# Tying a side chain's indirect transfers to the main chain's latest ScalarE instruction

## The chip, the cores and the metric

One Trainium2 chip; the kernel runs on one of its cores. The metric is device time in microseconds (us) of one execution. The kernel before takes 2101.95 us, the median of 15 runs (2098.95 to 2109.45).

## What is computed

Four layers on x of shape (4, 1024, 128), float32, each an attention-like part and a feed-forward part with a residual sum and a layer norm after each. Cut to what matters here:

```python
x = layernorm(x + L0_attn(x)); x = layernorm(x + L0_ffn(x))   # a scan; a quantised 128x128 product
x = layernorm(x + L1_attn(x))                                 # a linear state-space recurrence
x = layernorm(x + L1_ffn(x))      # 16 experts, 4 of them for each token, and a shared one
x = layernorm(x + L2_attn(x))     # causal softmax, 16 heads of 8
x = layernorm(x + L2_ffn(x))      # 8 experts, 2 for each token
x = layernorm(x + L3_attn(x))     # a Toeplitz mix with a gate
x = layernorm(x + L3_ffn(x))      # 32 experts, 4 for each token, and a shared one
```

An expert layer adds to each token the outputs of its chosen experts, each times a weight from the router.

## The kernel before

**Tiles.** The 4 x 1024 tokens lie in 32 tiles of 128 tokens in x, [128, 32, 128] in SBUF. Layer 1's experts take them in two halves, `a` and `r` (16 tiles each); layer 2's in `a2` (16), `m2` and `n2` (8 each); layer 3's in `a` (16), `b` and `c` (8 each).

**One expert layer.** The router's products give logits; `positions` (L1272 writes the result, `posl1r` and the like) gives each token the row that it has in a list sorted by expert. `spread` (L1303) copies every token's row of x to its places in that list in DRAM, named l1rr for layer 1, half r: for each tile and each of its k choices one indirect transfer of 128 rows of 512 bytes. 16 tiles with 4 choices are 64 transfers. The experts read the list in groups of four tiles (`gathered`, L1322; the load is L1326, on SP). Each load waits for all scatters of the list. Its tile xg is transposed on TensorE (L165, tp), multiplied with weights that lie in SBUF (L157, gu, yp), and the results go to a second list (l1yr). `collect` (L1350) gathers from that one: k indirect transfers fill a tile yt, and k VectorE instructions (L1361) add yt times the router's weight to x.

**Indirect transfers.** All are issued on GpSimd (POOL) by `indirect` (L1292; its instruction has line L1295), in the order in which they are emitted. `collect` keeps as many yt tiles as its pool has buffers (5 in layer 1, 8 in layers 2 and 3); a gather into a buffer waits for the adds that read it before. `moved_by` is the time at which the planner thinks that the transfers are over, 1.26 us for one.

**Who sets the order.** Stages are Python generators. One emits instructions and yields the time that it thinks they take. `mix(main, side)` (L233) takes a step of main, then steps of side until main's time is used up; when main has ended it emits all the rest of side, unless `drain=False`. `queued` (L223) emits one step of the side chain and puts an ordering "queued behind" on each of its instructions, behind main's latest one on the same engine (`self.latest`, of PE, ScalarE, VectorE and POOL). That is an order only and no wait: where an engine has none of main's work, its side work starts as soon as its data is there. POOL has none in the stages of this change. `run` (L217) adds the yields to `self.now`. In `collect` the adds of a tile are emitted when `self.now` has reached `moved_by` + 4.0, and where it has not, the generator yields 1.0 at a time.

**The stages that the change touches,** in order of time, in `all`:

- closing half a of layer 1 (`l1_close(a)`: gather, add, norm) beside the tail of half r's layers 0 and 1 (scans on VectorE, L645);
- **A**: `l2_attn(0)`, main, with `l1_route(r)` and the 64 scatters of l1rr at its side. Main's ScalarE work is the exponential (L1051, pr); L1057 masks pr on VectorE. Half r's experts come next, and with them eight wall loads for layer 2 (768 KB each, SP, L1437);
- **B**: half r's experts in layer 1, with layer 2's route of a2 and its 32 scatters (l2ra) at the side;
- **C**: layer 2's experts of a2, with `l1_close(r)` at the side: 64 gathers of l1yr in two quarters, adds, norm, transposes;
- `l2_attn(1)` and layer 2's other experts, with layer 2's gathers (`rows_in`) and layer 3's attention and route at the side;
- layer 3's experts of a, b, c. Beside those of a: `rows_in(m2)`, `rows_in(n2)`, `l3_attn(b)`, `l3_route(b)`, then the scatters of l3rb; main yields 9.0 for each block of its shared expert (L1652) and 3.7 for each group of the others (L1730). Behind l3rb stand on POOL the gathers of l3ya, the scatters of l3rc and the gathers of l3yb.

Of the kernel before, what the change touches and what calls it, by code (L numbers as in the profile page):

```python
# [56 lines left out]
class Part:  # L57
# [3 lines left out]
    def __init__(self, name, q0, nq, rows=None, lg0=None):  # L61
        self.name, self.q0, self.nq, self.lg0 = name, q0, nq, lg0
        if rows is None:
            self.order = list(range(q0 * QT, (q0 + nq) * QT))
        else:
            self.order = [tile_of(b, 2 * q + k) for b in rows for q in range(q0, q0 + nq) for k in range(2)]
        self.t0, self.nt = q0 * QT, len(self.order)
# [7 lines left out]
class Kernel:  # L75
    def __init__(self, ctx, tc, ins, out, cols, consts, rows):
        self.tc, self.nc, self.ins, self.out = tc, tc.nc, ins, out
        self.count = itertools.count()
        nc = self.nc
        self.const = self.pool(ctx, "const")  # L80
        self.small = self.pool(ctx, "small", 3)
        self.routes = self.pool(ctx, "routes")
        self.side = self.pool(ctx, "side", 2, space=PSUM)
        dram = self.pool(ctx, "dram", space=DRAM)

        self.cols_t = self.load(self.const, ins["cols"])
        self.cst_t = self.load(self.const, ins["consts"])
        self.x = self.tile(self.const, [P, NT, D], "x")
        self.xT = self.tile(self.const, [P, NT * P], "xT")
        nrow = ins["rows"].shape[1]  # L90
        self.rows_t = self.tile(self.const, [P, nrow], "rows")
        nc.gpsimd.dma_start(out=self.rows_t, in_=ins["rows"].to_broadcast([P, nrow]))
        self.col = {k: self.cols_t[:, a:b] for k, (a, b) in cols.items()}
        self.cst = {k: self.cst_t[:, a:b] for k, (a, b) in consts.items()}
        self.row = {k: self.rows_t[:, a:b] for k, (a, b) in rows.items()}
        self.ident = self.cst["ident"]
        self.eps = self.tile(self.const, [P, 1], "eps")
        nc.vector.memset(self.eps, LN_EPS)
        self.halfpi = self.tile(self.const, [P, 1], "halfpi")
        nc.vector.memset(self.halfpi, math.pi / 2)  # L100
        self.ones = self.tile(self.const, [P, E3], "ones")
        nc.vector.memset(self.ones, 1.0)
        self.mhalf = self.tile(self.const, [P, QT], "mhalf")
        nc.vector.memset(self.mhalf, -0.5)
        self.zero = self.tile(self.const, [P, D], "zero")
        nc.gpsimd.memset(self.zero, 0.0)
        self.flag = self.tile(self.const, [1, 1], "flag", I32)
        self.hm = self.tile(self.const, [P, 4], "hmg")

        self.first, self.rest = Part("a", 0, 2), (Part("b", 2, 1), Part("c", 3, 1))  # L110
        self.parts = (self.first, *self.rest)
        self.by_rows = (
            Part("a", 0, 2, range(B), 0), Part("m", 2, 2, (0, 1), NT // 2), Part("n", 2, 2, (2, 3), 3 * NT // 4)
        )

        self.rows_done = 0

        self.listed = set()

        self.traced, self.latest = nc.cur_bb.bb.instructions, {}  # L120
        self.now = self.moved_by = 0.0
        self.moved = []

        self.lists, self.route = {}, {}
        self.both = (self.first, Part("r", 2, 2))
        for lay, ne, k in (("l1", E1, K1), ("l2", E2, K2), ("l3", E3, K3)):
            for pt in {"l1": self.both, "l2": self.by_rows, "l3": self.parts}[lay]:
                tl = -(-((pt.nt * P * k + (P - 1) * ne) // P) // 4) * 4
                self.lists[lay, pt.name] = (
                    self.tile(dram, [tl * P, D], f"{lay}r{pt.name}"), self.tile(dram, [tl * P, D], f"{lay}y{pt.name}"), tl  # L130
                )
        self.wall2 = self.tile(dram, [P, E2 * 3 * F2], "wall2")
        self.xsave = self.tile(dram, [P, NT, D], "xsave")

        self.ksave = self.tile(dram, [P, B, BLK], "ksave")
        self.vsave = self.tile(dram, [P, B, 4, (NH + 1) * VW], "vsave")
# [85 lines left out]

    def queued(self, side):  # L223

        n = len(self.traced)
        got = next(side, None)
        behind = mybir.DependencyInfo(mybir.DependencyClass.NoSync, mybir.DependencyReason.DATA)
        for i in self.traced[n:]:
            if i.engine in self.latest:
                self.tc.add_manual_dep(i, self.latest[i.engine], behind, reason="queued behind")  # L230
        return got

    def mix(self, main, side, pace=1.0, drain=True):  # L233
# [1073 lines left out]
    def spread(self, lay, part, k):  # L1307

        pos, _, _, done = self.route[lay + part.name]
        rows = self.lists[lay, part.name][0]  # L1310
        for t in range(part.nt):
            for i in range(k):
                ins = self.indirect(
                    apart=done,
                    out=rows, out_offset=bass.IndirectOffsetOnAxis(ap=pos[:, t, i : i + 1], axis=0),
                    in_=self.x[:, part.order[t], :], in_offset=None,
                )
                done.append(ins)
            yield (1.26 * k,)
        self.listed.add(lay + part.name)  # L1320

    def gathered(self, pool, rows, g, done, want):  # L1322
# [27 lines left out]
    def collect(self, lay, part, k, yp, first=0, nt=None):  # L1350

        nc = self.nc
        pos, wk, _, _ = self.route[lay + part.name]
        assert f"made {lay}{part.name}" in self.listed
        ys = self.lists[lay, part.name][1]
        late = []

        def add():
            t, yt, _ = late.pop(0)
            for i in range(k):  # L1360
                nc.vector.scalar_tensor_tensor(  # L1361
                    self.x[:, part.order[t], :], yt[:, i, :], wk[:, t, i : i + 1], self.x[:, part.order[t], :],
                    ALU.mult, ALU.add,
                )

        for t in range(first, first + (nt or part.nt)):
            yt = self.tile(yp, [P, k, D], "yt")
            for i in range(k):
                self.indirect(
                    out=yt[:, i, :], out_offset=None, in_=ys,  # L1370
                    in_offset=bass.IndirectOffsetOnAxis(ap=pos[:, t, i : i + 1], axis=0),
                )

            late.append((t, yt, self.moved_by + 4.0))
            if len(late) == yp.bufs:
                while late[0][2] > self.now:
                    yield (1.0,)
                add()
            yield (1.26 * k,)
        while late:  # L1380
            while late[0][2] > self.now:
                yield (1.0,)
            add()
            yield (0.36 * k,)
# [439 lines left out]
    def all(self):  # L1824
# [4 lines left out]
        with ExitStack() as ctx:  # L1829
# [21 lines left out]
                    self.run(self.mix(self.abreast(self.l2_weights(), side), self.l1_close(a, yp)))  # L1851
            with ExitStack() as c2:
                wall = self.l1_wall(c2)
                self.run(self.mix(self.l2_attn(0), self.chain(self.l1_route(r), self.spread("l1", r, K1))))
                wall2 = self.l2_wall(c2)
                yp = self.pool(c2, "l1yr", 5, right=True)
                self.run(self.mix(self.chain(self.l1_experts(r, wall), self.l1_shared(r)), self.routed(a2)))
                self.run(self.mix(self.l2_experts(a2, wall2), self.l1_close(r, yp)))
            listed = lambda name: lambda: name in self.listed
            on = self.served(  # L1860
                self.chain(self.rows_in(a2), self.onward(a, True)),
# [212 lines left out]
```

## Time and profile before

| what | us or share |
|---|---|
| median of 15 runs | 2101.95 (2098.95 to 2109.45) |
| the profiled execution, its own time | 2102.99 |
| its span, first to last instruction | 2101.1 |
| mean granted TensorE clock | 0.888 |
| busy: PE, VectorE, ScalarE, POOL | 1625.9 (77%), 1344.2 (64%), 829.0 (39%), 777.1 (37%) |
| scatters of l1rr (64), first and last start | 704.9 and 787.7 |
| scatters of l2ra (32) | 869.4 to 908.5 |
| gathers of l1yr (64) | 922.6 to 1044.1 |
| scatters of l3rb (32) | 1804.7 to 1845.6 |

Times in the trace count from the span's start. A line of the chain of waits or of a timeline gives start, duration, engine, line, operation and tile; brackets give the idle time before it and what ended it. In a line of a group, the durations are minimum, median and maximum in ns, then follow the first and last start. "POOL" is GpSimd, "DVE" VectorE, "ACT" ScalarE, "SPq" SyncE's issues. An indirect transfer's time on POOL is the time that it keeps POOL; the data lands later.

### The profile page before, as it was taken

What the parts mean: (1) busy time and instruction counts of PE and PEld (TensorE: products, weight loads), DVE (VectorE), ACT (ScalarE), POOL (GpSimd) and SP (SyncE); (2) the same over time, 40 slices, a digit from 0 to 9 for tenths busy, and PEclk for the clock granted to TensorE, in tenths of its full rate; (3) what the DMA queues carried; (4) which work ended last, traced back from release to release, by engine and by line L of the source; (5) the groups of instructions that cost most, each with busy time, mean ns of one, the idle gap of its engine ahead of it and who ended that gap; (6) DMA issues with size and microseconds to landing.
All of it is one profiled execution on the core that took longest, in us unless ns stands there. A gap on an engine that the chain in (4) does not pass through costs nothing.

```text
span 2101.1 us, 28678 instructions
## 1 busy us (share of the span) xinstructions
PE 1625.9 (77%) x9605; PEld 1003.2 (48%) x9605; DVE 1344.2 (64%) x3801; ACT 829.0 (39%) x1193; POOL 777.1 (37%) x701
## 2 busy tenths in 40 slices
PE   6562677688848785999979787987989989788680
PEld 2232433377424343866643233333656678476470
DVE  8766699566666865645654756656583467778263
ACT  4720047233314352433327554663323254443140
POOL 5523148501660470353423000200216710477725
PEclk9775588899878997999989989999999999999895
DMA  9940000233451113432231000003115243155341
GB/s 308 286 124 0 1 19 34 95 96 105 148 175 42 44 67 138 142 116 73 80 124 30 1 1 1 20 2 136 51 47 210 62 129 109 64 140 142 104 136 51
DMA packets 225735, 192.05 MB, mean 91 GB/s; under 512 B 17008, under 2 KB 204272, under 8 KB 225072
## 3 DMA queue, kind: packets, MB, share of 16 engines
q1 hardware_dynamic: 204880, 147.28, 22.2%
q0 software_dynamic: 20704, 42.86, 6.7%
q8 instruction: 83, 1.36, 0.3%
q14 instruction: 68, 0.56, 0.1%
HBM read 93.47 MB, written 96.60 MB: 90 GB/s over the span
## 4 chain that ended last, share of the span: by engine, by line
PE 43%; DVE 17%; issue 7%; POOL 6%; DMA 4%; ACT 2%; SPq 0%; DVEq 0%; POOLq 0%; ACTq 0%
PE gu L157 13%; PE s L157 10%; PE yp L157 6%; PE sc L157 6%; PE tp L165 5%; POOL yt L1295 3%; DVE pr L1057 1%; POOL l3rb L1295 1%; ACT pr L1051 1%; POOL l3rc L1295 1%; PE s L165 1%; DVE x L205 1%; PE pu L157 1%; PE pg L157 1%; DVE y L1592 1%
## 5 line engine op out<-in xcount | busy, mean ns | idle before, releaser
L1051 ACT ACTIVATE pr<-sc 128x1024 f32<-128x1024 f32 x288 | 279.1, 1021 | 216.6 <-PE sc L157 212.1
L157 PE MATMUL gu<-ld,xgT 128*128 x768 | 197.7, 401 | 19.6 <-DVE hg L1693 13.3
L157 PE MATMUL sc<-qm,kT 32*128 32x512 f32 (+3 forms) x1536 | 188.8, 548 | 1.0 <-ACT pr L1051 1.0
L157 PE MATMUL s<-pr,va 128*32 128x512 f32 (+3 forms) x1536 | 163.1, 519 | 17.9 <-DVE x L989 7.3
L157 PE MATMUL gu<-wall,xgT 128*128 x352 | 169.7, 606 | 2.7 <-ACT xgT L167 2.0
L157 PEld LDWEIGHTS gu<-ld,xgT 128*128 128x128 f32 x768 | 143.6, 198 | 46.5 <-issue 10.4
L1057 DVE TENSOR_TENSOR pr<-pr,ld 128x512 f32<-128x512 f32 (+1 forms) x160 | 92.5, 581 | 84.7 <-ACT pr L1051 84.1
L1693 DVE TENSOR_TENSOR hg<-sg,gu 128x256 f32<-128x256 f32 x192 | 78.8, 417 | 105.7 <-ACT sg L1692 105.1
L169 DVE COPY hT<-tp 128x512 f32<-128x512 f32 x140 | 96.0, 686 | 64.7 <-PE tp L165 64.7
L167 ACT COPY xgT<-tp 128x512 f32<-128x512 f32 x118 | 69.0, 586 | 160.3 <-PE tp L165 160.3
L157 PEld LDWEIGHTS sc<-qm,kT 32*128 32x128 f32 x1536 | 82.7, 194 | 98.1 <-issue 60.2
L1692 ACT ACTIVATE sg<-gu 128x256 f32<-128x256 f32 x192 | 72.8, 383 | 142.3 <-PE gu L157 112.2
L165 PEld LDWEIGHTS tp<-ld,hg 128*128 128x128 f32 x736 | 92.3, 142 | 57.3 <-issue 37.6
L1295 POOL DMA_INDIRECT l1ra<-x,posl1a x64 | 94.6, 1478 | 61.0 <-DVE posl1a L1272 41.8
L1466 ACT ACTIVATE sg<-gu 128x512 f32<-128x512 f32 x88 | 52.5, 597 | 162.2 <-PE gu L157 158.6
L165 PE MATMUL tp<-ld,hg 128*128 128x128 f32 x736 | 113.7, 276 | 3.5 <-DVE hT L169 3.4
L157 PE MATMUL yp<-ld,hT 128*128 x768 | 102.5, 277 | 1.8 <-DVE mv L192 1.5
L1295 POOL DMA_INDIRECT l1rr<-x,posl1r x64 | 64.8, 1012 | 99.5 <-DVE posl1r L1272 80.3
L165 PE MATMUL tp<-ld,xg 128*128 128x128 f32 x472 | 76.6, 288 | 31.1 <-DMA xg<-l3rc 13.2
L1468 DVE TENSOR_TENSOR hg<-sg,gu 128x512 f32<-128x512 f32 x88 | 60.0, 682 | 57.0 <-ACT sg L1466 56.8
L157 PEld LDWEIGHTS yp<-ld,hT 128*128 128x128 f32 x768 | 94.1, 193 | 2.7 <-issue 2.0
L157 PE MATMUL yp<-wall,hT 128*128 x704 | 93.1, 276 | 1.5 <-DVE hT L169 1.5
(433 smaller groups left out, 3454.3 us busy)
## 6 DMA issues: line engine op xcount, KB each, us to landing
wall<-wall SPq DMA_DIRECT2D x16, 768.0 KB, 8.5
l3ra<-zero SPq DMA_DIRECT2D x1, 6144.0 KB, 30.4
ld<-in_l_w SPq DMA_DIRECT2D x2, 3072.0 KB
wall<-we SPq DMA_DIRECT2D x24, 256.0 KB, 2.0
ld<-in_l_w SPq DMA_DIRECT2D x1, 6144.0 KB, 20.4
xg<-l3ra SPq DMA_DIRECT2D x24, 256.0 KB, 2.8
l3ya<-yg SPq DMA_DIRECT2D x24, 256.0 KB, 2.3
l1ra<-zero SPq DMA_DIRECT2D x1, 5120.0 KB, 20.2
```

Source lines behind the costliest of these rows:

```text
L157: return self.nc.tensor.matmul(out, lhsT, rhs, start=start, stop=stop)
L165: nc.tensor.transpose(pt[:, k * P : (k + 1) * P], s, self.ident)
L167: nc.scalar.copy(dst, pt[:, : n * P])
L169: nc.vector.tensor_copy(dst, pt[:, : n * P])
L205: nc.vector.tensor_scalar(x, x, mv[:, t, 0:1], rstd[:, t : t + 1], ALU.subtract, ALU.mult)
L1051: nc.scalar.activation(pr, sc[h], AF.Exp)
L1057: nc.vector.tensor_tensor(d, d, cst["tril"].unsqueeze(1).unsqueeze(1).to_broadcast([P, 2, n, P]), ALU.mult)
L1295: ins = self.nc.gpsimd.indirect_dma_start(**kw)
L1466: nc.scalar.activation(sg, gu[:, 0, :], AF.Silu)
L1468: nc.vector.tensor_tensor(h, sg, gu[:, 1, :], ALU.mult)
L1692: nc.scalar.activation(sg, pg[:, :, 0, :], AF.Silu)
L1693: nc.vector.tensor_tensor(h[:, 2 * c : 2 * c + 2, :], sg, pg[:, :, 1, :], ALU.mult)
```

## The change

A flag `gated` is true during stages A, B and C. While it is, each indirect transfer that `queued` emits gets, besides its order, a real (semaphore) wait on the ScalarE instruction of main that was emitted last. And `spread` and `collect` now yield 1.26 after each transfer, everywhere in the kernel, where they yielded 1.26 k after the k transfers of a tile. In `collect` these yields stood behind the adds of an older tile; now they stand ahead of them.

```diff
@@ def queued(self, side):
         for i in self.traced[n:]:
             if i.engine in self.latest:
                 self.tc.add_manual_dep(i, self.latest[i.engine], behind, reason="queued behind")
+            if self.gated and i.name == self.moved[-1]:
+                after = mybir.DependencyInfo(mybir.DependencyClass.Sync, mybir.DependencyReason.DATA)
+                self.tc.add_manual_dep(i, self.latest[mybir.EngineType.Activation], after, reason="in step")
@@ def spread(self, lay, part, k):
                 done.append(ins)
-            yield (1.26 * k,)
+                yield (1.26,)
@@ def collect(self, lay, part, k, yp, first=0, nt=None):
                     in_offset=bass.IndirectOffsetOnAxis(ap=pos[:, t, i : i + 1], axis=0),
                 )
+                yield (1.26,)
...
                 add()
-            yield (1.26 * k,)
@@ def all(self):
+                self.gated = True
                 self.run(self.mix(self.l2_attn(0), self.chain(self.l1_route(r), self.spread("l1", r, K1))))
...
                 self.run(self.mix(self.l2_experts(a2, wall2), self.l1_close(r, yp)))
+            self.gated = False
```

The instructions, their number and POOL's order stay the same; ScalarE's, VectorE's and TensorE's instructions stand in another order from some points on.

More of the change, by code (lines that the diff above doesn't have):

```diff
@@ L1858, in all @@
                 self.run(self.mix(self.l2_experts(a2, wall2), self.l1_close(r, yp)))
+            self.gated = False
             listed = lambda name: lambda: name in self.listed
```

## The prediction

> **What bounds the kernel now.** I read the page first, then the chain of waits by stage, then the tiles that the change gates.
>
> ```profile
> span 2101.1 us, 28678 instructions
> ...
> ## 4 chain that ended last, share of the span: by engine, by line
> PE 43%; DVE 17%; issue 7%; POOL 6%; DMA 4%; ACT 2%; SPq 0%; DVEq 0%; POOLq 0%; ACTq 0%
> ```
>
> No engine bounds it alone; POOL is only 6% of the chain. So transfers matter where the chain crosses them, and the change must be priced stage by stage. First crossing: the lists of the second half of the tokens in layer 1 (l1rr), as the tile's view gives them.
>
> ```profile
> L1295 POOL DMA_INDIRECT l1rr<-x,posl1r x64: 954/958/1447, 704.9 to 787.7; - x64
> ...
>   PE tp L165: 10.4, 1
> ...
> DMA to landing us min/median/max: 2.7/2.8/13.7
> ```
>
> The 64 scatters start 1.26 us apart (0.96 busy, 0.30 issue), from 704.9 to 787.7, under the attention of layer 2. Who needs them is in the chain of waits at the end of that stage:
>
> ```profile
> 810.65 1.01 ACT pr L1051
> ...
> 820.71 0.70 DVE x L989
> 821.44 0.49 DVE bn L191 x2
> 825.31 15.03 DMA xg<-l1rr
> 840.38 1.97 PE tp L165 x8
> ```
>
> ScalarE's last pr of the stage ends at 812.6. The reads of l1rr (L1326) go out at 825.31 on SP, behind the eight 768 KB wall loads issued from 820.71, and land only at 840.4: between 819 and 837 the DMA view shows 380 to 430 GB/s in nearly every slice. So today the wall load ends that wait, and the scatters have landed 35 us early. PE has nothing else: 3.03 us busy in 825 to 840.
>
> Second crossing, layer 3, third quarter of rows (l3rb), from POOL's timeline and then the chain:
>
> ```profile
> 1804.65 0.99 POOL L1295 DMA_INDIRECT l3rb<-x,posl3b  x1 [111.84 <-DVE posl3b L1272]
> ```
> ```profile
> 1845.58 2.21 DMA l3rb<-x,posl3b
> ...
> 1972.18 2.92 DMA xg<-l3rc
> 1975.23 1.98 PE tp L165 x8
> ```
>
> POOL waits for the positions until 1804.65 and then works without a gap to 2012.7: 159.5 us of transfers (64 yt of l3ya, 32 l3rb, 32 l3rc, 32 yt of l3yb) and 48.6 us of idle, nearly all issue, fill the 208 us. The last quarter's experts wait for it at 1972. What delays posl3b delays the end.
>
> **Stage A (l2_attn(0) over the scatters of l1rr): +17.5 us.** The planner's yields, the number of transfers (64) and POOL's order stay. What is new is a real wait. Before, a scatter emitted late still ran early, since nothing on POOL held it. Now each waits for the ScalarE instruction that was main's latest when it was emitted. Following the emission: scatters 1 to 32 get pr instructions that end between 738.5 and 807.7 in the trace of before. From the 33rd on there is no newer one: 18 are emitted in main's last yields (projection, norm), which hold no ScalarE work, and 14 when main has ended. All 32 wait for the pr that ends at 812.6. Then they run in the burst: 32 x 1.264 = 40.4 us, the last begins near 851.8 and lands 2.8 later (median), 854.7. SP's reads wait for all 64; issue to landing is 2.8 (median of xg): the first tp comes at about 857.9 against 840.4, so +17.5. The wall load is by then over and hides nothing. Queued behind the waiting POOL instruction are only the scatters of l2ra (869.4 before), with positions that are themselves side work.
>
> Unknown: 13 to 16 of the 32 run beside the wall load; no row shows that pair. Low end: the quiet period, 1.264, and a read that lands 1 us sooner, 16.5. High end: the l1ra scatters, which averaged 1.478 busy against 1.012 for l1rr: 16 x 0.47 = 7.5 more, and a first read 2 us later: 27. I take the low row's period, since those of l1rr in the same stage are the nearest.
> A rule that speaks against the change: the Trainium skill ("DMA: Bandwidth & Descriptors", SWDGE vs HWDGE vs iDMA) says that each DMA engine takes turns between the queues fed by GpSimd and those fed by hardware. By it the scatters would pass a wall load in turn and only the wall, no longer last, would be late: the sum stays; l1ra's landings of up to 20.2 us beside other loads speak for less than that.
>
> Does the stage itself gain by thinner traffic? Split by whether a transfer runs beside it, the pr of L1057 takes 585 ns with and 578 without on average (median 681 both), L1051 1021 both. At 7 ns for 64 transfers, under 0.5 us: 0.
> The skill's "SBUF — State Buffer" (SBUF: two separate sides) has VectorE and GpSimd exclude each other on a shared port for whole instructions. If each of 64 transfers had held VectorE for its 0.96 us, 61 us would come back; the rows above show none of it, and it is POOL that is slowed (2.82 and 2.14 us beside two scans of L645 at 571 to 576).
>
> **Stage B (l2ra, 32 scatters): 0.** Gates end 6.7 to 12.3 us after the old starts, the last at 916.7; last landing near 922, its reader at 943.7. 20 us of cover.
>
> **Stage C (gathers of l1yr): +0.3 (0 to +5).** PE is 100% busy from 950 to 1050. The first quarter's gates reach 988.4, its adds stood at 998.6; second quarter's last gathers start near 1048.5, land at 1051, adds at 1053.6. Cover 1.3 to 2.7 us. If it fails, the norm and transposes slip one group, at most 5.
>
> **Yields after each transfer, everywhere: +7.2 us.** In `collect` the adds now come after the yields. Four places where that moves something:
> - Closing the first half in layer 1: a tile's four adds go from 562.7 behind both L645 scans (576.4), so POOL's gather of 569.92, which needs that buffer, starts near 576.6. It would have run beside the scans slowly anyway (2.82 and 2.14 instead of 0.94): net +1.7 (0 to +3.5). The chain runs along POOL there (564.9 to 623.6).
> - Start of l2_attn(1): one or two adds of l2ya less ahead of rot (a 9.8 us wait for yt): -1.
> - Layer 3, first quarter of experts (main) over rows_in, l3_attn(b), l3_route(b): the adds slip past main's 9.0 yields, so l3_attn(b) begins three main yields later (10 instead of 7), its route at 27 instead of 24. One such yield takes 3.54 us (gu groups at 1736.67, 1740.21): 10.6 later into the route, now 1782.5 to 1804.2, 21.7 us, of which some 8 are VectorE work of main interleaved. Positions are emitted after main's end, so part of the 8 falls away. posl3b is 4 to 11 later; I take +9, nearer the row of yields. Then POOL's gapless 208 us passes it on.
> - Last quarter of experts: adds of l3yb now hold VectorE ahead of main (PE stalls of 2.05 at 2011.65 and 1.58 at 2022.19, with 1.54 of waiting for yt); they come a group later: -2.5 (-4 to 0).
>
> 1.7 - 1 + 9 - 2.5 = +7.2.
>
> **Sum.** 17.5 + 0 + 0.3 + 7.2 = +25.0 on the profiled execution's 2102.99 us, 2128; that execution is 1.04 above the median of 2101.95, so 2127 for a median.
>
> **Rivals.**
> 1. Only the drained burst counts: layer 3's route makes up its delay (POOL's order has slack that I missed, or VectorE is freer). Against it: POOL shows no gap. 25 - 9 + 1 = +17: 2119.
> 2. The drained scatters collide with the wall load, +9.5 more: 2136.5; stage C's cover failing too, +5: 2142. For it: l1ra's slow scatters; against: the median landing of 2.8 in this stage.
> 3. Not slower: bursts cost the neighbours more than the rows say, through shared ports and DMA engines. Place: stages A to C, where 160 transfers are thinned. To cancel +25 each must give back 25/160 = 0.16 us of path; the rows show 0.007, at most 1.1 us. Priced at the break-even it gives 2102, and it decides from 0.16 us on.
> 4. The gate doesn't bind: if the tail of scatters were released before 812.6 (an earlier ScalarE instruction than I followed), up to 12 us later than now would still be hidden, and only the yields count: +7: 2109.
>
> **How the numbers follow.** Forecast (+25, 2120 to 2132) 0.50; rival 1 0.20; rival 2 0.17; rival 4 0.05; rival 3 0.08, half of it within 0.2% and half faster. 0.2%, about 4.2 us, is what a measurement here can tell from no change. Slower 0.91 with rival 4 mostly in it, same 0.05, faster 0.04. Range 2112 to 2142: low end 16.5 in stage A, nothing in layer 3, gains full (16.5 + 0 - 1 - 4 = +11.5, near 2113); high end 27 + 5 + 3.5 + 11 - 1 - 2.5 = +43, of which I keep +40.
>
> **What would show it.** Right: l1rr scatters to about 852 with an idle POOL that ends on ACT pr L1051, the first tp of l1rr near 858, all later starts moved by that; posl3b some 9 us later beyond the shift. l2ra and l1yr readers not waiting for POOL. Wrong: tp at 840 with scatters finished, a scatter period well above 1.3 after 820, L1057 shorter than 0.58, or PE waiting for adds between 990 and 1060.

## The result and the profile after

The changed kernel takes 2135.57 us (median of 9 runs, 2129.04 to 2143.81) against 2102.86 (47 runs of the kernel before): 1.0156 times, 95% interval 1.0142 to 1.0171, or +32.7. The prediction was 2127 and 2112 to 2142. The profiled execution took 2133.36, which is 30.4 above the one of before. In the lines shown, line numbers have moved by 1 to 5.

The page of the changed kernel:

```profile
span 2131.5 us, 28726 instructions
...
PE 35%; DVE 11%; issue 5%; POOL 4%; DMA 3%; ACT 2%; SPq 0%; DVEq 0%; POOLq 0%; ACTq 0%
```

Its shares of the chain add up to 60% (79% before), so the two can't be laid side by side. What can are the stages. The tile l1rr, and then the chain of waits behind stage A:

```profile
L1300 POOL DMA_INDIRECT l1rr<-x,posl1r x64: 953/958/1301, 741.1 to 856.3; - x64
...
  ACT pr L1056: 146.2, 9
...
  PE tp L166: 27.5, 1
...
DMA to landing us min/median/max: 2.7/2.7/3.4
```
```profile
856.34 2.21 DMA l1rr<-x,posl1r
858.55 0.02 SPq L1331
...
858.68 2.82 DMA xg<-l1rr
...
861.54 2.02 PE tp L166 x8
```

GpSimd waited 146 us for ScalarE's pr, and the last scatter begins at 856.3 instead of 787.7. What was a wait of 15 us behind the wall load is now a chain of the last scatter, its landing, SP's issue and the read of the list, each with nothing in between. (The row "DMA to landing" is that of the reads: the trace records no landing of a scatter of l1rr. The last one's, 2.21 us, is from the chain.) Layer 3's scatters of l3rb, GpSimd's timeline:

```profile
1834.72 0.99 POOL L1300 DMA_INDIRECT l3rb<-x,posl3b  x1 [120.16 <-DVE posl3b L1277]
```

They wait for posl3b, 120.16 us instead of 111.84. In closing half a of layer 1 a wait has appeared that the trace of before doesn't have. First the fifth and sixth gather of the row before, then the third to fifth after:

```profile
569.92 0.94 POOL L1295 DMA_INDIRECT yt<-l1ya,posl1a  x1 [0.30 <-DVE b L641]
571.17 2.82 POOL L1295 DMA_INDIRECT yt<-l1ya,posl1a  x1 [0.30 <-issue]
```
```profile
564.66 0.94 POOL L1300 DMA_INDIRECT yt<-l1ya,posl1a  x1 [0.30 <-issue]
565.91 0.94 POOL L1300 DMA_INDIRECT yt<-l1ya,posl1a  x1 [0.30 <-issue]
574.90 1.95 POOL L1300 DMA_INDIRECT yt<-l1ya,posl1a  x1 [8.05 <-DVE x L1366]
```

Where the 30.4 came from, by the shift of the same instruction between the two traces (median shift of TensorE's matmuls, GpSimd's transfers in layer 3):

| from here to there | shift at its ends | adds |
|---|---|---|
| start to 575 (no edit reaches it) | 0 to -2.9 | -2.9 |
| closing half a | -2.9 to +1.9 | +4.8 |
| inside stage A | +1.9 to +3.3 | +1.4 |
| end of stage A to the first tp of l1rr | +3.3 to +20.8 | +17.5 |
| stages B and C | +20.8 to +20.9 | 0 |
| l2_attn(1) to the scatters of l3ra | +20.9 to +21.1 | +0.2 |
| posl3b, first scatter of l3rb | +21.1 to +29.5 | +8.4 |
| GpSimd from l3rb to the gathers of l3yb | +29.5 to +33.1 | +3.6 |
| last experts | +33.1 to +29.8 | -3.3 |
| end | +29.8 to +30.4 | +0.6 |

The first row is what executions differ by before the change acts: in the traces below it lies between -6.6 and +3.9. So a trace's steps are read against its own shift just ahead of them, and totals from the medians. (Counted from the start of each span, the shifts from 575 on are all about 0.5 higher, so the first and the last row lose that much and no step between them changes.)

The step of closing half a hides a larger one: at 644 it stands at +8.0, and 3.1 of it come back between 652 and 664. What brings them back isn't shown; spread_new's trace below does the same there.

### The profile page after: what moved, and what is told of

It is laid out like the page before. It is cut to its first block, busy times and chain, and to the rows that moved or that the text cites. A ratio compares the mean times of both kernels' runs of the same rounds, so it can differ in the third digit from the quotient of the medians.

```text
span 2131.5 us, 28726 instructions
## 1 busy us (share of the span) xinstructions
PE 1625.1 (76%) x9605; PEld 1004.3 (47%) x9605; DVE 1343.2 (63%) x3801; ACT 829.7 (39%) x1193; POOL 776.7 (36%) x701
## 4 chain that ended last, share of the span: by engine, by line
PE 35%; DVE 11%; issue 5%; POOL 4%; DMA 3%; ACT 2%; SPq 0%; DVEq 0%; POOLq 0%; ACTq 0%
PE gu L158 11%; PE s L158 7%; PE yp L158 5%; PE tp L166 4%; PE sc L158 4%; POOL yt L1300 2%; POOL l3rb L1300 1%; POOL l3rc L1300 1%; PE pu L158 1%; PE pg L158 1%; PE py L158 1%; DVE x L206 1%; DVE y L1597 1%; DVE pr L1062 1%; PE s L166 1%
## 5 line engine op out<-in xcount | busy, mean ns | idle before, releaser
L158 PEld LDWEIGHTS gu<-ld,xgT 128*128 128x128 f32 x768 | 141.6, 195 | 53.6 <-issue 17.5
## 6 DMA issues: line engine op xcount, KB each, us to landing
wall<-wall SPq DMA_DIRECT2D x16, 768.0 KB, 12.8
l3ra<-zero SPq DMA_DIRECT2D x1, 6144.0 KB, 30.3
ld<-in_l_w SPq DMA_DIRECT2D x1, 6144.0 KB, 19.3
```

The costliest lines, as they stand in the source:

```text
L158: return self.nc.tensor.matmul(out, lhsT, rhs, start=start, stop=stop)
```

## The experiments

The theory was: two separate costs, a burst of drained scatters behind stage A, and the order that the yields make. Rivals: the wait itself costs everywhere; stage C's cover fails; or bursts of transfers cost their neighbours more than the rows said. The first four kernels ran beside a kernel before that took 2529.44 us (18 runs), 20% more than elsewhere; I call them set S. The eight others ran where it takes 2102.59 and 2101.86. The record gives the chip of all twelve the same number, 11, so it is not shown whether set S was another chip or the same one in another condition; where an expectation below says "chip", this is open. Gains and losses in us are the ratio less one, times the kernel before of that set. "Drained" are the scatters that wait for the last pr of the stage.

**yields_only**, set S: `gated` stays False.

```diff
-                self.gated = True
+                self.gated = False
```

> The per-transfer yields stay, no transfer is gated. My theory: the cost of the change is two separate sums, a burst of 32 gated scatters behind stage A and a new order of the adds. Without the gate the first tp of l1rr is back at about 840 to 844, and what is left is the order alone: the prediction's steps gave +7, the steps of the changed kernel's trace give about +13 (4.8 in closing half a, 8.4 at posl3b, 4 more on POOL behind it, -3.3 in the last experts). Rival: the cost is the wait itself, everywhere it stands; then this kernel is within 4 us of the kernel before.

Measured: 1.0072 (1.0042 to 1.0101).

**gate_only**, set S: the kernel before with the flag, and yields as before. A tile's transfers come in one step there, so all of them are gated.

```diff
+            if self.gated and i.name in self.moved[-4:]:
```

> The gates of stages A, B and C stay, the yields are those of the kernel before (one for a tile's transfers, adds ahead of them). My theory: +17 to +18 alone, with l1rr's last scatter near 852 and its first tp near 858; closing half a and posl3b stand as before. Rival (the cost is the new order of the adds, the burst is hidden): within 4 us of the kernel before. The two alone should add up to the whole change, about 30, if they are independent.

Measured: 0.9669 (0.9623 to 0.9715), 84 us faster. That is neither theory's answer.

**gate_bc**, set S: the changed kernel with `self.gated = True` one line later, behind stage A.

> As the changed kernel, but the gate begins with stage B, so that stage A's scatters run free. My theory: gates in B and C cost nothing, so the time is that of yields_only within 2 us. Rival: stage C's thin cover (1.3 to 2.7 us by the prediction) fails, 2 to 5 us above yields_only, with PE waiting for layer 1's adds around 1000 to 1060.

Measured: 0.9952 (0.9926 to 0.9977), 33 us less than yields_only, where my theory had the two equal.

**quick**, set S: the changed kernel with

```diff
+                quick = ((0.6,) for _ in self.spread("l1", r, K1))
-                self.run(self.mix(self.l2_attn(0), self.chain(self.l1_route(r), self.spread("l1", r, K1))))
+                self.run(self.mix(self.l2_attn(0), self.chain(self.l1_route(r), quick)))
```

> As the changed kernel, all gates in place, but a scatter of stage A counts 0.6 instead of 1.26 for the planner, so that all 64 are emitted while main still has ScalarE work; the last gate is a pr that ends at 807.7 in the trace of before. My theory: only the 32 that hang on the stage's last pr cost time. The scatters now end near 824, ahead of the wall load's end, the first tp of l1rr is at 843 to 845 and the time is that of yields_only within 2 us: 17 us less than the changed kernel. Rival (waiting on ScalarE in step, or scatters beside main's end and beside the wall load, cost time in themselves): most of the 17 us stays.

Measured: 0.9824 (0.9781 to 0.9867), 66 us less than yields_only, where my theory had the two equal. In set S every kernel with more gates is faster than one with fewer. The table by stretches of stage A of yields_only (columns: length, busy time of PE, PEld, DVE, ACT, POOL, granted clock, DMA share, GB/s), TensorE's timeline in it, and the longest piece of the chain of waits there:

```profile
712.00:732.00 20.00, 13.15 (x112) 6.08 (x113) 18.80 (x80) 4.90 (x5) 10.87 (x12) 0.83 0.09 34
...
755.00:798.00 43.00, 5.38 (x11) 1.28 (x10) 0.00 (x0) 0.00 (x0) 32.65 (x35) 0.50 0.13 52
798.00:830.00 32.00, 20.18 (x141) 9.16 (x145) 13.43 (x26) 10.89 (x12) 0.69 (x1) 0.71 0.08 30
```
```profile
763.73 0.37 PE L158 MATMUL s<-pr,va 128*32 128x128 f32 x1 [2.00 <-issue]
766.52 0.37 PE L158 MATMUL s<-pr,va 128*32 128x128 f32 x1 [2.43 <-issue]
769.33 0.37 PE L158 MATMUL s<-pr,va 128*32 128x128 f32 x1 [2.43 <-issue]
```
```profile
750.12 57.76 another core or an unknown queue
```

While the burst of scatters lasts (717.8 to 797.7), VectorE and ScalarE do nothing for 43 us and TensorE one matmul in 2.8 us, with "issue" before it; the DMA engines are 13% busy. What VectorE waits for there the profile can't name (57.76 us). When the last scatter has gone all run again. The same kernel in yields_only_b below, where the kernel before takes 2102.59, same stretch of the scatters:

```profile
755.00:791.00 36.00, 28.94 (x282) 13.97 (x282) 26.39 (x71) 18.12 (x19) 27.46 (x29) 1.00 0.19 75
```

Counted over the whole trace, the time in which TensorE, VectorE and ScalarE are all idle while GpSimd issues transfers (pauses under 1 us between them included) is 348 us in yields_only and 85 in yields_only_b; 120 and 63 when it issues none. gate_bc differs from yields_only by the gates of B and C alone and has 298; gate_only, with all gates and the old yields, has 263. So in set S the others nearly stop during a burst, and waiting in step relieves it. It is not shown what they lack; neither the changed kernel nor a trace of the kernel before was taken there. The Trainium skill ("Runtime: NRT & Kernel Launch", Instruction fetch mechanics) says that each engine's sequencer fetches its next instructions over a DMA queue of its own while it executes, and that the cost is mostly hidden. In the 43 us above the trace has one packet of the instruction queues, in the 36 us of yields_only_b three; that would fit starved fetching, but engines that execute little also fetch little, so it proves nothing.

The next four, where the kernel before takes 2102.59:

**yields_only_b**, the same kernel as yields_only.

> The same kernel as yields_only. In the first call the kernel before itself took 2529 us, with 57 us and more in which no engine but GpSimd worked while scatters ran, and the two halves of the change read +0.7% and -3.3%. Two theories now. Drain theory: on a chip where the kernel before takes about 2102 the order of the adds alone costs +13 (1.006), by the steps of the changed kernel's trace. Starvation theory (bursts of indirect transfers hold up every engine): belongs to the chip of the first call; there it reads 1.007 again.

Measured: 2116.23, 1.0061 (1.0039 to 1.0084): +12.8, as the drain theory had it.

**gate_only_b**, the same kernel as gate_only.

> The same kernel as gate_only. Drain theory: where the kernel before takes about 2102, +17 to +18 (1.008), l1rr's first tp near 858. Starvation theory: where it takes about 2529, 0.967 again.

Measured: 2121.20, 1.0092 (1.0074 to 1.0110): +19.3. The two halves add up to 1.0153, the whole measured 1.0159 beside them. Chain of waits:

```profile
848.24 2.22 DMA l1rr<-x,posl1r
...
850.58 2.76 DMA xg<-l1rr
853.38 2.06 PE tp L166 x8
```

The shift goes from -4.9 to +12.4 here, +17.3, and stays at 12.0 to 12.4 to the end: stages B and C cost nothing (TensorE busy 118.42 of the 120 us from 940, 118.25 before).

**quick_gate**: gate_only, and the scatters of stage A at half their time.

```diff
+                quick = ((0.5 * g[0],) for g in self.spread("l1", r, K1))
```

> As gate_only, but a scatter of stage A counts half for the planner, so that all 64 get a gate ahead of the stage's last pr. Drain theory, where the kernel before takes about 2102: the 17 us are gone, within 3 us of the kernel before, with the scatters over by 825 and the first tp near 841. Starvation theory, where it takes about 2529: denser scatters starve the other engines longer, so slower than gate_only by 10 us or more but still faster than the kernel before.

Measured: 2100.33, 0.9993 (0.9981 to 1.0005). All gates in place, and the cost is gone:

```profile
817.54 6.23 DMA l1rr<-x,posl1r
823.89 12.07 DMA xg<-l1rr
836.01 1.97 PE tp L166 x8
```

Here the last scatter does lie beside the wall load: it lands in 6.23 us instead of 2.2, and the wall load ends last again. None hangs on the last pr; nine still start behind its end at 807.5, and they are hidden. It is not the wait that costs, but the number of scatters left behind the last ScalarE instruction.

**after_again**, the changed kernel.

> The changed kernel itself, beside the others on one chip. Drain theory, where the kernel before takes about 2102: 1.014 to 1.017 again, the sum of yields_only_b and gate_only_b. Starvation theory, where it takes about 2529: the gate's gain outweighs both costs, between gate_only's 0.967 and 0.98 (0.967 plus the 0.7% that the yields alone cost there).

Measured: 2137.02, 1.0159 (1.0142 to 1.0176). Its trace records the landing of every fourth or so of the scatters; the issues from 832 to 848, beside the wall load, and from 852 to 866, behind it (KB each, median us to landing):

```profile
wall<-wall SPq DMA_DIRECT2D x8, 768.0 KB, 12.3
l1rr<-x,posl1r POOLq DMA_INDIRECT x14, 6.0
```
```profile
l1rr<-x,posl1r POOLq DMA_INDIRECT x11, 2.2
```

**spread_new**: the kernel before with only `spread`'s edit.

```diff
-            yield (1.26 * k,)
+                yield (1.26,)
         self.listed.add(lay + part.name)
```

> The kernel before with one edit: spread yields after each transfer. No gate, collect as before. Theory A (the prediction's): the delay of posl3b comes from collect's adds, which slip past main's yields of 9.0; then this kernel shows no delay at posl3b and stands within 3 us of the kernel before. Theory B: it comes from the scatters of l3ra. The step of the side chain that is emitted while layer 2's experts have not begun holds one scatter now instead of four, so three transfers (3.8 us for the planner) are left over, the list ends two main yields later (25 instead of 23, the last of that stage), and l3_attn(b) begins at main yield 10 instead of 7 of the next stage: posl3b 8 us later, the end 8 to 12 later (1.004 to 1.006). All for a kernel before of about 2102.

Measured: 2110.09, 1.0041 (1.0024 to 1.0057): +8.6. **collect_new** has `collect`'s edit only.

> The kernel before with the other half of the yields: collect yields after each transfer, ahead of the adds; spread as before, no gate. Theory A: posl3b 8 us later, the whole of the yields' +13. Theory B: posl3b as in the kernel before; closing half a costs 5 to 6 (POOL waits some 8 us there for an add behind two scans), the last experts give 2.5 back, the sum +2 to +4 (1.001 to 1.002). With spread_new it should add up to the +13 of yields_only_b.

Measured: 2110.19, 1.0042 (1.0026 to 1.0058): +8.8, more than the +2 to +4 of theory B. The two add up to 1.0083, where yields_only_b had 1.0061 (1.0039 to 1.0084). The tiles l3ra and l3rb (first and last start): l3ra before, both of spread_new, both of collect_new:

```profile
L1295 POOL DMA_INDIRECT l3ra<-x,posl3a x64: 952/958/1154, 1565.2 to 1651.8; - x64
```
```profile
L1295 POOL DMA_INDIRECT l3ra<-x,posl3a x64: 952/958/1269, 1562.0 to 1648.6; - x64
L1295 POOL DMA_INDIRECT l3rb<-x,posl3b x32: 954/958/1349, 1810.8 to 1850.4; - x32
```
```profile
L1300 POOL DMA_INDIRECT l3ra<-x,posl3a x64: 952/958/1154, 1572.1 to 1658.8; - x64
L1300 POOL DMA_INDIRECT l3rb<-x,posl3b x32: 954/958/3266, 1810.9 to 1853.3; - x32
```

From the last scatter of l3ra to the first of l3rb are 162.2 us in the one and 152.1 in the other; before it was 152.9 (1804.65 less 1651.8). So posl3b's delay (+9.3) comes from `spread` and theory B holds. In closing half a it is the other way round. GpSimd's timelines, spread_new first:

```profile
563.88 0.94 POOL L1295 DMA_INDIRECT yt<-l1ya,posl1a  x1 [0.31 <-DVE b L641]
565.13 2.83 POOL L1295 DMA_INDIRECT yt<-l1ya,posl1a  x1 [0.30 <-issue]
568.27 2.14 POOL L1295 DMA_INDIRECT yt<-l1ya,posl1a  x1 [0.30 <-issue]
```
```profile
566.84 0.94 POOL L1300 DMA_INDIRECT yt<-l1ya,posl1a  x1 [0.30 <-issue]
575.84 1.94 POOL L1300 DMA_INDIRECT yt<-l1ya,posl1a  x1 [8.05 <-DVE x L1366]
```

collect_new shows the 8.05 us wait again, and its shift goes from -1.8 to +6.6 there (+8.5, not the 5 to 6 expected); spread_new's ends where it began, at -6.6. At the last experts, from 2002 to 2026, collect_new gets 3.2 back; spread_new, without that edit, 1.8.

**dose**: as quick_gate with 0.8 for 0.5.

> As gate_only, but a scatter of stage A counts 0.8 of its time for the planner: 40 of the 64 get a gate ahead of the stage's last pr and 24 hang on it, where gate_only had 32 and quick_gate none. Drain theory: 24 x 1.264 = 30.3 us behind that pr instead of 40.4, so 10.1 less than gate_only: last scatter near 838 on the clock of gate_only's trace, first tp near 843.3 against 853.4 there, and +9 against a kernel before of about 2102 (1.004). If what costs is waiting as such and not the number left over, it stays at gate_only's +17 to +19.

Measured: 2110.80, 1.0037 (1.0019 to 1.0055): +7.8, 11.5 less than gate_only_b. In the trace the step behind stage A is +6.9 (3.7 to 10.6), 10.4 less than gate_only_b's 17.3, for 8 scatters less: 1.30 each, about a scatter's period. (Its trace runs 8.6 later than gate_only_b's into this stage, so clock times don't compare.)

**best**: quick_gate, with `collect`'s edit in layer 3 only.

```diff
+                if lay == "l3":
+                    yield (1.26,)
...
-            yield (1.26 * k,)
+            if lay != "l3":
+                yield (1.26 * k,)
```

> quick_gate with collect's yields ahead of the adds in layer 3 only (closing half a and layer 2's gathers as before). By the traces the last experts gain 2.5 and nothing else moves: 2 to 4 us below a kernel before of about 2102 (0.998 to 0.999). Where the kernel before takes about 2529, near quick_gate's place: faster than it by 1.5 to 3.5%.

Measured: 2104.32, 1.0009 (0.9992 to 1.0026): no gain. The last experts give 4.4 back (-1.6 to -5.9), but about 3 are lost ahead of them, after 1800 (-4.4 to -1.6). That loss isn't the edit's: quick_gate's trace, without it, loses 2.4 there too. From 2002 to 2026 best gets 2.8 back and quick_gate 1.4. No kernel here beats the kernel before where that takes 2102; quick_gate is level with it.

## Why the prediction was right, and where not

- **Stage A, +17.5: right,** mechanism and size: 17.5 in the changed kernel, 17.3 with the gate alone, 6.9 with 24 scatters left and none with 0. The 32 take 40.4 us at 1.264 each, of which 23 are hidden under what follows the last pr; of the 30.3 of 24 scatters 23 are hidden as well. So each scatter beyond some 18 costs its period (an estimate from these two kernels). That the sum came out within 0.2 is partly luck: two misses cancel. The first drained scatter starts 0.74 after the pr's end, and the last lands after 2.21 instead of 2.8.
- **The collision with the wall load (rival 2)** happens and costs nothing. The drained scatters of the changed kernel took 961 ns of GpSimd on average and started 1.27 us apart. In after_again's trace the four with a recorded landing between 832.6 and 846.5, beside the load, landed after 5.36 to 7.25 us, the three behind them after 2.21 to 2.22: the last scatter is issued when the load is over. In quick_gate the slow landing (6.23) is hidden behind the load.
- **The landings in the prediction aren't those of scatters.** The trace of before records none for l1rr and l1ra: the median of 2.8 is that of the reads on SP, and the 20.2 at l1ra is that of the zeros written at 17.2 us. So neither is evidence for or against rival 2.
- **Stages B and C, 0 and +0.3: right.**
- **posl3b, +9: right in size** (8.4, and 9.3 with `spread`'s edit alone), **wrong in its cause.** The failed sentence is "the adds slip past main's 9.0 yields". collect_new has those adds and no delay. It is the scatters of l3ra that bring it; how, I read from the order of the emission: ahead of layer 2's last experts the side chain is pressed on until "routed l3a" is listed, and the step that shows it held four scatters and holds one. Three are left, 3.8 us for the planner, the list ends two main yields later, and the rest of the side chain starts later by three. The order of the emission gave the number right; I attached the wrong reason to it.
- **Closing half a, +1.7 (0 to +3.5): mis-sized.** It is +4.8 in the changed kernel's trace and +8.4 in yields_only_b's and collect_new's; at 644 the four traces with that edit stand at +8.0 to +9.1, the five without it at +0.1 to +2.7. I let the wait take the place of the transfers that the scans slow down, and so counted 5.0 us as saved. GpSimd's wait came as foreseen, at the gather that needs that buffer, 8.05 us long; its row of gathers from first to last grew from 96.7 us by 8.1 in the changed kernel, where nothing was saved, and by 5.7 in collect_new, where some 2 us were.
- **GpSimd behind l3rb, 0: missed,** +3.6. It lies in the gathers of l3ya: they grow by 4.1 us, of which 2.3 are longer transfers and most of the rest a wait of 2.0 for adds. In spread_new, where the row also starts late, they grow by 3.5, all of it longer transfers; in collect_new by 1.1. So a later start can bring most of it; what makes single gathers longer there isn't shown.
- **Last experts, -2.5: right in size** (-3.3). From 2002 to 2026 the five traces with that edit get 2.8 to 3.2 back, but of the four without it spread_new 1.8 and quick_gate 1.4, so only a part is shown to be the adds'. Start of l2_attn(1), -1: -0.5.
- **Rivals 1 and 4** fall: layer 3 doesn't make up its delay (+8.4), and the gate binds (146 us of waiting for pr).
- **Rival 3 (bursts cost the neighbours)** is wrong where the kernel before takes 2102: the gate alone loses 19.3 us, and quick_gate, all gates and no drained scatters, gains 4 at most. In set S the gate alone gains 84. The profile of before showed no sign of it, as it was taken where the effect doesn't appear.

The forecast 25.0 against 32.7: closing half a (+3 to +7) and GpSimd's row behind l3rb (+3.6) are the difference, as far as the traces tell. In stage A itself after_again lost 5.9 and the changed kernel's profile 1.4, beside dips of the granted clock (0.74 and 0.83 from 760 to 780, 1.00 in yields_only_b); whether the gate brings the dips is not shown.

## What to carry to other kernels

A wait that ties side work to the main chain is free only for what is issued while that chain still runs: count what is left when its last instruction of that engine has gone, multiply by the period, and take off what other waits hide (here 23 us). Pacing in a planner's units moves more than what it paces: follow each changed yield to the next place where the planner stops at a mark or a full buffer. And take a gain from "no bursts", or a loss, as that of the conditions it was measured in until it has been seen in others.

## What the runs showed that I had not expected

- In set S the kernel before takes 2529 us instead of 2102. In yields_only's trace there all engines but GpSimd nearly stop during a burst of indirect transfers, with the DMA engines at 13%; the same gates that cost 0.9% elsewhere gain 3.3% there. The cause is open.
- An indirect scatter's landing went from 2.2 to 6.23 us beside 6 MB of wall loads (quick_gate; 5.36 to 7.25 in after_again), while its time on GpSimd stayed at 0.96 (median; 1.37 at most).
